# One-hots of queries made by two passes on ScalarE in place of one on VectorE

## The chip, the cores and the metric

The kernel runs on one core of one Trainium2 chip. The metric is the device time of one execution in microseconds (us). Before the change it is 1225.16 us, the median of 14 runs that lie between 1217.1 and 1229.05.

In the profile PE is TensorE (PEld its weight loads), DVE is VectorE, ACT is ScalarE, POOL is GpSimd and SP is SyncE, which issues most of the transfers. Each engine works its own queue of instructions in the order in which the kernel wrote them, and waits on semaphores for data and for free buffers.

## What is computed

One layer of a graph network over 3125 nodes of 128 features and 100000 edges, each of one of 5 types. The edges are sorted by their destination `dst`. For every type r and each of 8 heads:

```
q = x[dst] @ W_Q[r];  k = x[src] @ W_K[r];  v = x[src] @ W_V[r]
logits = (q * k).sum(-1) / 4 + attn_bias[r]            # only edges of type r
attn   = exp(logits - max over the edges of one dst) / (sum over the edges of one dst)
out   += sum over the edges of one dst of attn * v
```

`out` goes through a projection, is added to x and normalised over the features; the result is added to x once more and normalised again.

## The kernel before, in words

**Tables.** In a set-up of about 90 us the kernel makes, per node and type, the keys and values (kv_d) and for the first nodes the queries (q_d, each query as three bf16 parts) in DRAM. It also writes key_d: for every edge its key, 5 times the destination's place in a window plus the type. `row_of` is a column that holds the number of each partition.

**Groups.** The edges are worked in 196 groups of 512 (four tiles of 128 edges). The destinations of a group lie in a window of 25 nodes, so 125 pairs of node and type. A one-hot matrix `hot` of 125 rows by 512 edges says which pair each edge belongs to. A product of `hot` with the window's queries (qw) gives every edge its query (qe); a second product with the window's maxima (mw) gives every edge its maximum. A second one-hot, `at`, with edges along the partitions, sums weighted values over the pairs.

**Steps.** A loop in Python runs over steps k and writes the instructions of all engines in a fixed order; nothing is reordered later. In step k the stages stand for different groups, and the letters v and g name the later and the earlier front of the work:

- SP loads the keys kt (L367, three buffers) and the queries qw (L373) of group k + 3, and mw (L853) for groups whose maxima are due. POOL gathers keys and values of the edges with four indirect transfers a group (L681, into 22 buffers).
- ACT: `by_node` (L949) puts finished sums into place, `carry` copies a window's sums to pt (L930), parts of new queries are cast (L702, L712, L722), `exps` (L876) makes the exponentials, `weights` (L889) and `types` (L753) copy small columns, and `places` makes `at`: four passes of Abs with a bias column (L901) and one Relu over all four tiles (L904).
- PE: `spread_m` (L863) gives the edges their maxima, `sums` (L915, L917 for the carried part from pt, L924) sums, `spread_q` (L746) gives the edges of group k + 1 their queries.
- DVE: `weigh` (L881) weighs values, `less_max` (L872) subtracts the maxima, `norm` (L936 den, L937, L939) divides, `logits` (L759, L760) multiplies queries and keys, and `spot` (L737) makes `hot` of group k + 2 with one comparison of kt against `row_of`. `hot` has 21 buffers, since the same one-hot is used again when the maxima are known, 19 steps later for most groups.

**Blocks.** The maxima are made for blocks of 128 nodes. About every eight steps the logits of a block are complete. POOL loads them by node (ell, L772). ACT turns them to by_head (L787), DVE makes the maxima in three steps (wl at L810, mx at L816, the bf16 parts up to L831). They are stored to m_d (L839) and come back as mw. Once a block also come the projection (L956, L957), the residual and norms on DVE (L974 to L1007), and on ACT the square root (L982), which lies between two loads of ACT's function table.

In the order of a step `spot` stands after `logits`, and `places` after `spot`. The last parts of a step are the parts of queries on DVE (L726, L717), the maxima (with by_head on ACT), the projection and the square root.

Of the kernel before, what the change touches and what calls it, by code (L numbers as in the profile page):

```python
# [11 lines left out]
AF = mybir.ActivationFunctionType  # L12
ALU = mybir.AluOpType
# [33 lines left out]
WR = WN * R  # L47
# [67 lines left out]
def block_of(g, ends=tuple(P * (b + 1) for b in range(NT))):  # L115

    return min(
        b for b, n in enumerate(ends)
        if n >= N or E // N * n - slack(n) >= min(E, (g + 1) * GE)
    )  # L120
# [12 lines left out]
def windowed_path(  # L133
# [4 lines left out]
    nc = tc.nc  # L138
# [90 lines left out]
    def iota(name, pattern, n, base=0, mult=0, dt=F32, pool=const):  # L229
        t = pool.tile([P, n], dt, name=name)  # L230
        nc.gpsimd.iota(
            t, pattern=pattern, base=base, channel_multiplier=mult,
            allow_small_or_imprecise_dtypes=True,
        )
        return t

    node = iota("node", [[P, NT]], NT, mult=1)
    row_of = iota("row_of", [[0, 1]], 1, mult=1)
    row_at = iota("row_at", [[1, P]], P)
    step = iota("step", [[1, P]], P, mult=-1, pool=load)  # L240
    slot = iota("slot", [[1, D]], D)
# [20 lines left out]
    off = load.tile([1, NT], F32, name="off")  # L262
# [89 lines left out]
    live = {}  # L352
# [12 lines left out]
    def fetch_keys(g):  # L365
        kt = ahead.tile([P, T, P], BF16, name="kt")
        nc.sync.dma_start(kt.rearrange("w t p -> w (t p)"), key_d[g].partition_broadcast(P))  # L367
        live["kt", g] = kt

    def fetch_q(g):  # L370
        qw = ahead.tile([P, 3, H], BF16, name="qw")
        f = window(g, first5, SPE)
        nc.sync.dma_start(qw.rearrange("w s h -> w (s h)"), q_d[bass.ds(f, P), :])  # L373
        live["qw", g] = qw
# [303 lines left out]
    def gather(g):  # L678
        kv = kvs_[g % KVB]
        for t in range(T):  # L680
            nc.gpsimd.indirect_dma_start(  # L681
                out=kv[:, t, :], out_offset=None, in_=kv_d[:, :],
                in_offset=bass.IndirectOffsetOnAxis(ap=idx[:, t, g : g + 1], axis=0),
            )


    def fetch_x(name, b):
        n = min(P, N - b * P)
        xb = flow.tile([P, H], F32, name=name, bufs=2 if name == "xq" else 3)
        if n < P:  # L690
            nc.vector.memset(xb, 0.0)
        nc.sync.dma_start(xb[:n], x[b * P : b * P + n, :])
        live[name, b] = xb
# [34 lines left out]
    def store_q(b):  # L728
        live.pop(("xT", b))
        nc.sync.dma_start(  # L730
            q_d[b * P * R : (b + 1) * P * R, :].rearrange("(p r) c -> p (r c)", r=R),
            live.pop(("q3", b)).rearrange("p r s h -> p (r s h)"),
        )

    def spot(g):
        hot = hold.tile([WR, T, P], BF16, name="hot")
        nc.vector.tensor_scalar(hot, live.pop(("kt", g))[:WR], row_of[:WR], None, op0=ALU.is_equal)  # L737
        live["hot", g] = hot

    def spread_q(g):  # L740
# [23 lines left out]
    def store_logits(g):  # L764
        nc.sync.dma_start(
            lg_d[g * GE : (g + 1) * GE, :].rearrange("(p t) c -> p (t c)", t=T),
            live["lg", g].rearrange("p t c -> p (t c)"),
        )
# [81 lines left out]
    def fetch_m(g):  # L850
        mw = late_flow.tile([P, 2, 3, HEADS // 2], BF16, name="mw", bufs=4)
        f = window(g, first5, SPE)
        nc.sync.dma_start(mw.rearrange("w h s k -> w (h s k)"), m_d[bass.ds(f, P), :])  # L853
        live["mw", g] = mw
# [36 lines left out]
    def places(g, on_dve):  # L891

        at = late_flow.tile([P, T, WR], F32, name="at", bufs=3)
        for t in range(T):
            if t < on_dve:
                nc.vector.tensor_scalar(
                    at[:, t, :], row_at[:, :WR], nkey[:, t, g : g + 1], 0.0,
                    op0=ALU.add, op1=ALU.is_equal,
                )
            else:  # L900
                nc.scalar.activation(  # L901
                    at[:, t, :], row_at[:, :WR], AF.Abs, bias=nkey[:, t, g : g + 1], scale=1.0
                )
        nc.scalar.activation(at[:, on_dve:], at[:, on_dve:], AF.Relu, bias=1.0, scale=-1.0)  # L904
        live["at", g] = at
# [21 lines left out]
    def carry(g):  # L927
        if g < NGR - 1:
            pt = late_flow.tile([WR, PW], F32, name="pt")
            nc.scalar.copy(pt, live["pp", g])  # L930
            live["pt", g] = pt
# [15 lines left out]
    def by_node(g):  # L947
        f = window(g, first, ACTE)
        nc.scalar.copy(oT[:, bass.ds(f, WN)], live.pop(("op", g)))  # L949
# [63 lines left out]
    def store_z(b):  # L1013
        n = min(P, N - b * P)
        nc.sync.dma_start(out[b * P : b * P + n, :], live.pop(("z", b))[:n, :])
# [7 lines left out]
    final = step_of[NGR - 1]  # L1023
# [9 lines left out]
    at_k, k = {}, 0  # L1033
    for v in range(NGR):
        k = max(k + 1, ready[block_of(v, MEND)])
        at_k[v] = k
    v_at = {k: v for v, k in at_k.items()}
# [24 lines left out]
    for k in range(-2, root_at[NT] + 2):  # L1062
        v, g = v_at.get(k), group_at.get(k)
        q_step = {k - f: b for b, f in enumerate(q_from) if b >= QB and -2 <= k - f <= 5}

        if k >= 0 and k + 3 in group_at:
            fetch_keys(group_at[k + 3])
            fetch_q(group_at[k + 3])
        if -2 in q_step:
            fetch_x("xq", q_step[-2])  # L1070
        for b in range(NT):
            if done_at[b] - 1 == k:
                fetch_x("xr", b)
            if norm_at[b + 1] + 1 == k:
                store_z(b)
        if 5 in q_step:
            store_q(q_step[5])
        for u in range(NGR):
            if max(at_k[u] - 3, ready[block_of(u, MEND)] - 2) == k:
                fetch_m(u)  # L1080

        while gathered < NGR - 1 and step_of[gathered + 1] <= k + (AHEAD if k < final - 16 else 1):
            gathered += 1
            gather(gathered)
        for b in range(NM):
            if full_step[b] + 1 == k:
                maxima_load(b)

        for b in range(NT):
            if done_at[b] + 1 == k:  # L1090
                residual(b)
        if v_at.get(k - 4) is not None:
            by_node(v_at[k - 4])
        if v_at.get(k - 2) is not None:
            carry(v_at[k - 2])
        if 1 in q_step:
            turned(q_step[1])
        if 3 in q_step or 4 in q_step:
            second_part()
        if 2 in q_step or 3 in q_step:  # L1100
            first_part()

        if v_at.get(k + 1) is not None:
            spread_m(v_at[k + 1], 8 if k + 1 in group_at else 12)
        if v_at.get(k - 1) is not None or v_at.get(k - 3) is not None:
            sums(v_at.get(k - 1), v_at.get(k - 3))
        if k + 1 in group_at:
            spread_q(group_at[k + 1])

        if v is not None:  # L1110
            weigh(v)
        if v_at.get(k + 1) is not None:
            less_max(v_at[k + 1])
            exps(v_at[k + 1])
        if v is not None:
            weights(v)
        if k + 1 in group_at:
            types(group_at[k + 1])
        if v_at.get(k - 2) is not None:
            norm(v_at[k - 2])  # L1120
        if g is not None:
            logits(g)
            store_logits(g)
        if k + 2 in group_at:
            spot(group_at[k + 2])
        if v_at.get(k + 1) is not None:
            places(v_at[k + 1], 2 if k >= final - 1 else 0)
        if 3 in q_step or 4 in q_step:
            third_part()
        if 2 in q_step or 3 in q_step:  # L1130
            remainder()
        for b in range(NM):
            whole = MB[b][2] is None
            last = ready[b] - (3 if whole else 4)
            if last - 2 == k and whole:
                maxima(b, 0, 2)
            if last - 1 == k and whole:
                maxima(b, 2, 4)
            if last == k:
                maxima(b, 4 if whole else 0, R)  # L1140
                store_m(b)
        for b in range(NT):
            if done_at[b] == k:
                project(b)
        for b in range(NT + 1):
            if root_at[b] == k:
                roots(b)
            if norm_at[b] == k:
                norms(b)
        if 0 in q_step:  # L1150
            turn_q(q_step[0])
        if 1 in q_step:
            queries(q_step[1], 0, RH)
        if 2 in q_step:
            queries(q_step[2], RH, R)
# [505 lines left out]
```

## Time and profile before

| | |
|---|---|
| Median of 14 runs | 1225.16 us |
| The profiled execution's own time | 1217.63 us |
| Its span, first to last instruction | 1215.8 us |
| Granted clock of TensorE, mean | 0.804 |
| hot on DVE (L737) | 196, mean 370 ns, 72.4 us busy |
| Abs of places on ACT (L901) | 744, 125 elements each, mean 398 ns |
| Relu of places on ACT (L904), 500 elements | 176, mean 620 ns |
| Gathers on POOL (L681) | 784, mean 950 ns |

A row of a group of instructions gives their number, the time that they kept the engine busy, the mean time of one, and the idle time of the engine just ahead of them with what ended it. A row of a wait gives who waited for whom, the total in us, how many times and the longest. The chain of work that ended last is followed back from the last instruction; its shares say on which engine the time of that one chain was spent, which differs from busy time.

### The profile page before, as it was taken

Reading aid. Unit: us, or ns where it says so; the run is one execution under the profiler, and the core shown is the slowest. Engines: PE = TensorE matmul, PEld = TensorE weight load, DVE = VectorE, ACT = ScalarE, POOL = GpSimd, SP = SyncE. Lnnn points to the kernel's source line nnn. Section 1 sums busy time; section 2 is a strip of 40 time slices with the busy share of each in tenths; the row PEclk is TensorE's granted clock in tenths of the full one; section 3 lists DMA queues with packets and bytes.
Section 4 is the critical chain, followed back from the end, with each engine's and each line's share of the span. In section 5 each row is a group of like instructions: output and inputs, shape, how many; then the busy total and the mean of one; then the engine's idle time right before and its main releaser. Section 6 shows DMA issues by size and latency. Waiting matters only on the chain.

```text
span 1215.8 us, 25674 instructions
## 1 busy us (share of the span) xinstructions
PE 839.6 (69%) x7526; PEld 659.2 (54%) x7526; DVE 931.4 (77%) x2559; ACT 631.1 (52%) x2248; POOL 799.8 (66%) x901
## 2 busy tenths in 40 slices
PE   7984345766667776776678677667767866866794
PEld 3543234655555565565556565546546655655573
DVE  4654377689778878877887897788788788778786
ACT  2560024455664664665565466466556545655453
POOL 1627777777777777776777777777776777667200
PEclk9995558778977888888797878789788778777797
DMA  6887677666766776776676667666666657666300
GB/s 168 323 328 203 165 166 178 180 164 161 193 170 166 179 174 154 171 187 163 161 183 171 154 171 183 162 164 179 171 163 173 180 146 175 174 143 155 73 7 19
DMA packets 180889, 203.63 MB, mean 167 GB/s; under 512 B 83207, under 2 KB 146083, under 8 KB 180620
## 3 DMA queue, kind: packets, MB, share of 16 engines
q0 software_dynamic: 40896, 113.39, 34.1%
q1 hardware_dynamic: 135414, 83.80, 28.4%
q10 hardware_dynamic: 4430, 4.71, 1.6%
q8 instruction: 63, 1.03, 0.3%
q14 instruction: 86, 0.70, 0.2%
HBM read 166.50 MB, written 35.28 MB: 166 GB/s over the span
## 4 chain that ended last, share of the span: by engine, by line
DVE 26%; PE 24%; DMA 17%; ACT 10%; issue 10%; POOL 9%; SPq 3%; ACTq 0%; DVEq 0%; POOLq 0%
POOL kv L681 8%; PE pp L915 8%; DMA mw<-m_d 8%; DMA kv<-kv_d,idx 5%; DVE wl L810 4%; PE pr L395 4%; PE me L863 4%; ACT at L901 4%; DVE prod L759 3%; DVE wv L881 3%; DVE lg L760 3%; DVE mx L816 3%; PE qe L746 2%; DMA qw<-q_d 2%; PE pp L917 2%
## 5 line engine op out<-in xcount | busy, mean ns | idle before, releaser
L681 POOL DMA_INDIRECT kv<-kv_d,idx x784 | 744.9, 950 | 264.3 <-issue 197.3
L915 PE MATMUL pp<-wv,at 128*125 128x136 f32 x1568 | 344.3, 352 | 1.3 <-DVE o L939 1.3
L915 PEld LDWEIGHTS pp<-wv,at 128*125 128x125 f32 x1568 | 258.0, 228 | 60.7 <-issue 58.5
L901 ACT ACTIVATE at<-row_at,nkey 128x125 f32<-128x125 f32 x744 | 237.6, 398 | 0.0
L863 PE MATMUL me<-mw,hot 125*128 125x64 bf16 (+1 forms) x2352 | 124.0, 208 | 152.4 <-DMA mw<-m_d 109.6
L746 PE MATMUL qe<-qw,hot 125*128 125x128 bf16 x2352 | 196.4, 244 | 37.1 <-DVE hot L737 33.4
L876 ACT ACTIVATE me<-me 128x32 f32<-128x32 f32 x196 | 35.7, 182 | 343.9 <-DVE me L872 343.6
L863 PEld LDWEIGHTS <-hot 125*128 125x128 bf16 x2352 | 110.0, 107 | 182.2 <-issue 106.3
L746 PEld LDWEIGHTS <-hot 125*128 125x128 bf16 x2352 | 182.8, 118 | 43.1 <-DVE hot L737 41.1
L759 DVE TENSOR_TENSOR prod<-kv,qe 128x512 f32<-128x512 f32 x196 | 133.0, 679 | 48.8 <-DMA kv<-kv_d,idx 47.0
L760 DVE TENSOR_REDUCE lg<-prod 128x32 f32<-128x512 f32 x196 | 134.4, 686 | 6.8
L881 DVE TENSOR_TENSOR wv<-kv,me 128x512 f32<-128x512 f32 x196 | 132.5, 676 | 3.9 <-PE pp L915 3.9
L917 PE MATMUL pp<-pt,carried 125*5 125x136 f32 x390 | 90.2, 319 | 58.4 <-ACT pt L930 56.5
L904 ACT ACTIVATE at<-at 128x500 f32<-128x500 f32 (+1 forms) x196 | 117.3, 599 | 6.2
L707 PE MATMUL prq<-wq,xTq 128*128 128x384 f32 (+1 forms) x88 | 47.0, 627 | 91.3 <-DVE rem L717 91.3
L872 DVE TENSOR_TENSOR me<-lg,me 128x32 f32<-128x32 f32 x196 | 37.4, 191 | 75.8 <-PE me L863 67.5
L810 DVE TENSOR_TENSOR wl<-by_head,shut 128x1024 f32<-128x1024 f32 (+2 forms) x73 | 76.9, 1053 | 11.0 <-ACT by_head L787 8.5
L816 DVE TENSOR_REDUCE mx<-wl 128x16 f32<-128x1024 f32 (+2 forms) x73 | 76.5, 1048 | 2.5
L924 PEld LDWEIGHTS pp<-rsum,o 125*128 125x128 f32 x392 | 74.5, 232 | 4.1 <-issue 4.0
L737 DVE TENSOR_SCALAR hot<-kt,row_of 125x512 bf16<-125x512 bf16 x196 | 72.4, 370 | 1.5 <-DMA kt<-key_d 1.0
L917 PEld LDWEIGHTS pp<-pt,carried 125*5 125x5 f32 x390 | 18.2, 86 | 97.2 <-ACT pt L930 74.9
L924 PE MATMUL pp<-rsum,o 125*128 125x25 f32 x392 | 67.8, 255 | 3.9 <-DVE o L939 3.9
(184 smaller groups left out, 984.8 us busy)
## 6 DMA issues: line engine op xcount, KB each, us to landing
kt<-key_d SPq DMA_DIRECT2D x196, 128.0 KB
qw<-q_d SPq DMA_DIRECT2D x196, 96.0 KB
kv_d<-kvs SPq DMA_DIRECT2D x24, 640.0 KB
kv<-kv_d,idx POOLq DMA_INDIRECT x784
q_d<-q SPq DMA_DIRECT2D x22, 480.0 KB
lg_d<-lg SPq DMA_DIRECT2D x196, 18.0 KB
mw<-m_d SPq DMA_DIRECT2D x196, 6.0 KB
xr<-in_x SPq DMA_DIRECT2D x24, 64.0 KB
```

Of the source, the lines that this page charges most:

```text
L681: nc.gpsimd.indirect_dma_start(out=kv[:, t, :], out_offset=None, in_=kv_d[:, :], in_offset=bass.IndirectOffsetOnAxis(ap=idx[:, t, g : g + ...
L746: nc.tensor.matmul(qe[:, t, :], hot[:, t, :], qw[:WR, s, :], start=(s == 0), stop=(s == 2))
L759: nc.vector.tensor_tensor(prod, kv[:, :, :H], live.pop(("qe", g)), op=ALU.mult)
L760: nc.vector.tensor_reduce(lg[:, :, :HEADS], prod.rearrange("p t (k d) -> p t k d", d=HD), AX.X, ALU.add)
L810: nc.vector.tensor_tensor(wl, by_head[:, None].to_broadcast([P, n, nh, D]), shut[:, :n, None, :].to_broadcast([P, n, nh, D]), op=ALU.add,)
L863: nc.tensor.matmul(me[:, t], hot[:, t, :], mw[:WR, None, :, s, :].to_broadcast([WR, times, 2, HEADS // 2]), start=(s == 0), stop=(s == 2),)
L881: nc.vector.tensor_tensor(wv[:, :, :H].rearrange("p t (k d) -> p t k d", d=HD), kv[:, :, H:].rearrange("p t (k d) -> p t k d", d=HD), live ...
L901: nc.scalar.activation(at[:, t, :], row_at[:, :WR], AF.Abs, bias=nkey[:, t, g : g + 1], scale=1.0)
L904: nc.scalar.activation(at[:, on_dve:], at[:, on_dve:], AF.Relu, bias=1.0, scale=-1.0)
L915: nc.tensor.matmul(pp, at[:, t, :], wv[:, t, :], start=(t == 0), stop=(t == T - 1))
L917: nc.tensor.matmul(pp[:R], carried[:WR, g, :], live.pop(("pt", g - 1)), start=False, stop=False,)
L924: nc.tensor.matmul(op, live.pop(("o5", done)), rsum[:WR], start=True, stop=True)
```

## The change

`spot` of the first two groups stays as it is, on DVE. From the third group on ACT makes `hot` with two passes. The first overwrites kt with |kt - row|: Abs with the new column `row_neg`, minus the number of the partition, as bias. The second writes Relu(1 - |kt - row|) to `hot`: keys and rows are whole numbers, so that this ramp is 1 at the target and 0 elsewhere. In the order of a step `places` now stands ahead of `spot`, so that on ACT the pair follows the five passes of `places`.

```diff
     row_of = iota("row_of", [[0, 1]], 1, mult=1)
+    row_neg = iota("row_neg", [[0, 1]], 1, mult=-1)
...
     def spot(g):
         hot = hold.tile([WR, T, P], BF16, name="hot")
-        nc.vector.tensor_scalar(hot, live.pop(("kt", g))[:WR], row_of[:WR], None, op0=ALU.is_equal)
+        off = live.pop(("kt", g))[:WR]
+        if g < 2:
+            nc.vector.tensor_scalar(hot, off, row_of[:WR], None, op0=ALU.is_equal)
+        else:
+            nc.scalar.activation(off, off, AF.Abs, bias=row_neg[:WR], scale=1.0)
+            nc.scalar.activation(hot, off, AF.Relu, bias=1.0, scale=-1.0)
         live["hot", g] = hot
...
             store_logits(g)
+        if v_at.get(k + 1) is not None:
+            places(v_at[k + 1], 2 if k >= final - 1 else 0)
         if k + 2 in group_at:
             spot(group_at[k + 2])
-        if v_at.get(k + 1) is not None:
-            places(v_at[k + 1], 2 if k >= final - 1 else 0)
         if 3 in q_step or 4 in q_step:
```

## The prediction

> **What bounds the kernel now.** I read the page first, for shares and the chain; then the waits by size; then one block's instructions in order of time on ACT, DVE and PE.
>
> From the page:
>
> ```profile
> span 1215.8 us, 25674 instructions
> PE 839.6 (69%) x7526; PEld 659.2 (54%) x7526; DVE 931.4 (77%) x2559; ACT 631.1 (52%) x2248; POOL 799.8 (66%) x901
> DVE 26%; PE 24%; DMA 17%; ACT 10%; issue 10%; POOL 9%; SPq 3%; ACTq 0%; DVEq 0%; POOLq 0%
> ```
>
> DVE is the busiest engine, but it carries only 26% of the chain: no engine bounds the kernel alone, the chain goes round all of them. Next, the waits (who waited for whom: us in total, times, longest):
>
> ```profile
> ACT me L876 <- DVE me L872: 343.6, 170, 7.6
> POOL kv L681 <- issue: 197.3, 647, 0.5
> PEld pp L917 <- ACT pt L930: 74.9, 82, 2.3
> DVE prod L759 <- DMA kv<-kv_d,idx: 47.0, 19, 5.5
> DVE den L936 <- ACT pt L930: 14.9, 19, 1.2
> DVE wl L810 <- ACT by_head L787: 8.5, 22, 0.4
> ```
>
> ACT waits 343.6 us for DVE, so on the average it has room. But three rows have somebody waiting for ACT, and two of them come about once a block of nodes (19 and 22 times for 25 blocks). POOL's row says that its gathers run back to back, 0.95 + 0.30 us each: 784 + 25 of them fill 1011 of the 1045 us from 89.1 to 1134.8, which leaves 34 us to be won at most. Now ACT in the block that ends at 648 us (start us, us, instruction, idle time before it):
>
> ```profile
> 612.95 0.18 ACT L876 ACTIVATE me<-me 128x32 f32<-128x32 f32 x1 [1.61 <-DVE me L872]
> ...
> 614.51 0.62 ACT L904 ACTIVATE at<-at 128x500 f32<-128x500 f32 x1
> ...
> 615.86 0.18 ACT L876 ACTIVATE me<-me 128x32 f32<-128x32 f32 x1 [0.27 <-DVE me L872]
> ...
> 618.04 1.28 ACT L982 ACT_TABLE_LOAD   x1
> ...
> 619.60 0.27 ACT L930 COPY pt<-pp 125x136 f32<-125x136 f32 x1
> 619.89 1.28 ACT L876 ACT_TABLE_LOAD   x1
> ...
> 624.43 0.18 ACT L876 ACTIVATE me<-me 128x32 f32<-128x32 f32 x1 [0.83 <-DVE me L872]
> ...
> 625.99 0.62 ACT L904 ACTIVATE at<-at 128x500 f32<-128x500 f32 x1
> 626.52 1.07 ACT L787 COPY by_head<-ell 128x512 f32<-128x512 f32 x1
> ```
>
> and DVE and PE in the same block:
>
> ```profile
> 619.90 0.17 DVE L936 TENSOR_SCALAR den<-pp 125x8 f32<-125x8 f32 x1 [0.77 <-ACT pt L930]
> ...
> 627.62 1.23 DVE L810 TENSOR_TENSOR wl<-by_head,shut 128x1024 f32<-128x1024 f32 x1 [0.44 <-ACT by_head L787]
> ...
> 642.01 0.20 DVE L831 TENSOR_TENSOR m<-mx,m 128x40 bf16<-128x40 f32 x1
> ...
> 648.34 0.80 PE L863 MATMUL me<-mw,hot 125*128 125x64 bf16 x12 [3.31 <-DMA mw<-m_d]
> ```
>
> From 612.95 to 627.6 ACT works almost without a gap: exps and places of four steps, the square root between two table loads, then by_head. DVE waits for its end (0.44), makes the maxima until 642.2, they go out and back as mw, and PE (3.31 idle) starts the next block on them at 648.3. So these four steps of ACT are on the path, once a block.
>
> **The change, part by part.** *Removed:* 194 of 196 one-hots on DVE. One takes 0.34 us and delays what follows by 0.26 (next start less its own, 632.65 to 632.91). Between 627.6 and 642.0 there are two on the path: -0.52 us a block. In the four steps before, DVE waits for ACT anyway, and in the two after, PE waits for mw: nothing.
>
> *Added:* a pair of passes on ACT a step. The second, Relu of 512 elements, is priced by the places' Relu of 500: 0.620, so 0.63. The first has a bias column; the nearest row is the count's Sign (250 elements, bias column, 0.506), and the places' 250 and 500 rows (0.412, 0.620) give 0.83 ns an element, so 0.506 + 262 x 0.00083 = 0.72. Between a pass and the one that reads it lie 0.03 us (L901's end to L904), and an unrelated successor starts 0.09 before the end (625.99 + 0.53). A pair delays ACT by 0.72 + 0.03 + 0.54 = 1.29 us. Bounds: 1.06 (two at L904's pitch, 0.53) and 1.40 (0.72 twice less overlap); I take 1.29, nearest to both kinds of pass.
>
> The Trainium skill (ScalarE: Activation LUTs, Rules for kernel authors) sends relu-like work to VectorE and calls DVE "up to about 3× faster in bf16". By that ratio alone a pass would be an estimated 3 x 0.34 = 1.03 us, a pair 2.06, and the block sum below 6.6 instead of 3.5 us. I go by the rows, which put one pass at about twice DVE's one-hot.
>
> *On the path, block 605 to 648:* delay after the first step 1.29; the idle 0.27 at 615.86 takes some back, 1.02; after the second step 2.31. That goes through the table load and square root into pt at 619.60, and DVE, which waits there already, waits 2.31 more. After the third step 3.60. At 624.43 the idle 0.83 goes: DVE's own part comes 2.31 - 0.26 later and is still ahead of ACT; 2.77. After the fourth step 4.06, which by_head and then DVE's wl take in full. Less 0.52: **+3.5 us in this block**. Called a sum: 4 x 1.29 - 1.10 - 0.52. The same sum on the rows of the blocks whose by_head ends at 456.7, 584.9, 843.4 and 1017.9 gives 3.3, 2.4, 3.3 and 1.6; the mean of the five is 2.8. In the other four steps the waits of L876 for DVE (2.80, 2.86, 2.15, 2.72) hide the pair, as long as they stay over 1.29.
>
> Seventeen blocks (by_head from 413.6 to 1099.2) have this form: 17 x 2.8 = 48. Five before have POOL still behind: DVE waits there for kv (9.8 and 2.4 us in the first two) and covers the delay; in the other three I count 2 each, 6. The last block's wl doesn't wait for by_head. Sum: **+54 us**.
>
> *The rest, together:* The constant's iota on POOL (another of that shape took 0.12) lies in the set-up, before the gathers at 89 us. The move of spot behind places changes ACT's order alone: on DVE's queue places has work only from the step where no spot is left. The new waits on ACT are those that spot had on DVE, with by_node, pt and exps of the next step queued behind: for kt, loaded a step and more ahead (DVE waited for it once, 1.0 us), and for hot's buffer. No DMA is issued by spot. It frees kt for SP's load three groups on, and SP has two steps for that. The buffer of hot is that of 21 groups before, whose last readers on PE ended at least 6.2 us before the places of that step. PE's wait for hot can't be longer than the one for pt, which ACT now makes just after the pair and PE needs ahead of it. The first 15 steps have no places: ACT idles and POOL sets the pace, so nothing. The last 20 have no spots.
>
> Own time of the profiled run: 1217.6 (span 1215.8 and 1.8 around it), so 1272; it is one of the lowest of 14 and the median is 7.5 above it: **1225 + 54 = 1279 us**.
>
> **Rivals.** (a) *Faster: DVE's relief counts and ACT has room.* For it: 77% against 52% busy, and 343.6 us of ACT waiting for DVE. The Trainium skill (Perfetto Trace Analysis, Identifying the Most-Contended Engine) says to optimise the engine of highest occupancy first; by that all 194 x 0.344 would count, an estimated -67 us. The gathers leave only 34. If the pairs are hidden, the three one-hots on the chain of a block go (those at 614.78, 632.65, 638.31: 0.26 each), 0.78 x 22 = 17: 1208 us. It decides if a pair is under (1.10 + 0.52) / 4 = 0.4 us; against it, one bf16 cast of 384 elements takes 0.51 on ACT. (b) *Slower, less:* the pair is at its lower bound, and PE, less pressed, gets a clock over the present 0.80, which shortens its pieces of the chain (some 9 us a block) by 5%: 17 x (2.8 - 0.8 - 0.45) + 6 = 32, some 1240 to 1257. (c) *Slower, more:* pairs of the later steps come out too, because pt late holds PE (82 waits already) and that holds qe and DVE. One more pair a block is 17 x 1.29 = 22: 1301; all four would be 88: 1367. Against it: those idle times of 2 to 3 us. (d) *The change doesn't do what it says:* the two functions could need table loads of their own; the places use both 940 times between exps without one, so I leave it at nothing.
>
> **How the numbers follow.** Main case 0.70, with its own range 1260 to 1300 (pair 1.06 to 1.40, and 1.6 to 3.5 us a block); (b) 0.08; (c) 0.13, mostly under 1325; (a) 0.07; no change 0.02. The range 1243 to 1318 holds the main case, most of (b) and two thirds of (c). Within 0.3%, about what a measurement of this kernel tells from no change, only a chance meeting of (a) and (b) would fall.
>
> **What would show it.** Right: two ACT rows in place of L737, near 0.72 and 0.63 us, 194 each; DVE's wait at wl for by_head up from 0.4 to about 4 us a time, and at den for pt from 0.8 to about 3; the gap from one by_head to the next up from some 43 us to 46; POOL idle for freed buffers. DVE's busy time falls by 67 us and ACT's rises by some 250, to about 70%. Wrong: wl's wait under 1 us, or a pair well under 1 us (then a or b); L876 no longer waiting in the later steps (then c).

## The result, and the profile after

| | before | after |
|---|---|---|
| Median of the runs | 1224.43 us (47 runs, 1216.51 to 1232.24) | 1271.55 us (10 runs, 1268.05 to 1274.84) |
| Ratio, 95% interval | | 1.0389 [1.0367, 1.0411] |
| Profiled execution, own time | 1217.63 us | 1279.67 us |
| Its span | 1215.8 us | 1277.9 us |

The kernel became 47 us slower. The two profiled executions lie 62 us apart: that of before is one of the fastest of its kernel, that of after lies above all ten runs. For that reason the differences that are read from the two traces add up to 62 us and not to the 47 of the medians. Line numbers of the loop are 1 to 6 higher after the change.

The page after:

```profile
span 1277.9 us, 26125 instructions
PE 882.9 (69%) x7526; PEld 697.1 (55%) x7526; DVE 881.1 (69%) x2365; ACT 862.8 (68%) x2636; POOL 799.6 (63%) x902
DVE 20%; PE 19%; DMA 19%; ACT 18%; POOL 11%; issue 10%; SPq 2%; ACTq 0%; DVEq 0%; POOLq 0%
L742 ACT ACTIVATE kt<-kt,row_neg 125x512 bf16<-125x512 bf16 x194 | 137.2, 707 | 21.8 <-DMA kt<-key_d 19.8
L743 ACT ACTIVATE hot<-kt 125x512 bf16<-125x512 bf16 x194 | 122.1, 630 | 6.1
```

DVE is 50 us less busy and ACT 232 us more; the four engines' shares are now nearly alike, none is over 70%, and the kernel is slower. ACT's share of the chain went from 10% to 18%. The waits after (who waited for whom: us in total, times, longest):

```profile
ACT me L882 <- DVE me L878: 256.5, 130, 7.0
POOL kv L682 <- issue: 199.9, 654, 0.6
PEld pp L923 <- ACT pt L936: 170.1, 102, 3.3
DVE den L942 <- ACT pt L936: 82.6, 61, 2.5
POOL kv L682 <- DVE den L942: 56.3, 42, 3.9
DVE prod L765 <- DMA kv<-kv_d,idx: 49.9, 20, 5.3
DVE wl L816 <- ACT by_head L793: 38.8, 22, 3.0
ACT kt L742 <- DMA kt<-key_d: 19.8, 9, 4.0
```

The three rows in which somebody waits for ACT grew from 74.9 to 170.1, from 14.9 to 82.6 and from 8.5 to 38.8 us. DVE alone waits 98 us more for ACT, and POOL now waits 56 us at den, which is DVE's place in its queue when it is late in freeing gather buffers (10.5 us before). The last row is new: ACT waits nine times for the keys, each time ahead of 166 us, when the gathers hold DVE up too.

Now ACT in the block whose by_head ends at 658.9 us (start us, us, instruction, idle time before it):

```profile
640.49 0.18 ACT L882 ACTIVATE me<-me 128x32 f32<-128x32 f32 x1 [1.60 <-DVE me L878]
...
642.05 0.62 ACT L910 ACTIVATE at<-at 128x500 f32<-128x500 f32 x1
642.58 0.71 ACT L742 ACTIVATE kt<-kt,row_neg 125x512 bf16<-125x512 bf16 x1
643.31 0.63 ACT L743 ACTIVATE hot<-kt 125x512 bf16<-125x512 bf16 x1
...
644.27 0.20 ACT L882 ACTIVATE me<-me 128x32 f32<-128x32 f32 x1
...
647.75 1.28 ACT L988 ACT_TABLE_LOAD   x1
...
649.60 1.28 ACT L882 ACT_TABLE_LOAD   x1
...
654.47 0.20 ACT L882 ACTIVATE me<-me 128x32 f32<-128x32 f32 x1
...
656.57 0.70 ACT L742 ACTIVATE kt<-kt,row_neg 125x512 bf16<-125x512 bf16 x1
657.31 0.63 ACT L743 ACTIVATE hot<-kt 125x512 bf16<-125x512 bf16 x1
657.84 1.06 ACT L793 COPY by_head<-ell 128x512 f32<-128x512 f32 x1
```

and DVE in the same block:

```profile
644.41 0.17 DVE L942 TENSOR_SCALAR den<-pp 125x8 f32<-125x8 f32 x1 [1.31 <-ACT pt L936]
...
649.61 0.17 DVE L942 TENSOR_SCALAR den<-pp 125x8 f32<-125x8 f32 x1 [2.41 <-ACT pt L936]
...
654.62 0.17 DVE L942 TENSOR_SCALAR den<-pp 125x8 f32<-125x8 f32 x1 [0.77 <-ACT pt L936]
...
658.94 1.23 DVE L816 TENSOR_TENSOR wl<-by_head,shut 128x1024 f32<-128x1024 f32 x1 [1.70 <-ACT by_head L793]
...
672.63 0.20 DVE L837 TENSOR_TENSOR m<-mx,m 128x40 bf16<-128x40 f32 x1
```

The idle times at 615.86 and 624.43 (0.27 and 0.83) are gone: their counterparts, the exps at 644.27 and 654.47, start with no wait. From the first exps to the end of by_head the stretch takes 658.90 - 640.49 = 18.41 us, before 627.59 - 612.95 = 14.64: 3.77 longer. DVE waits four times in it, 6.19 us together, before twice, 1.21. From by_head's end to the end of the maxima it is 672.83 - 658.90 = 13.93, before 14.62: 0.69 shorter; the two one-hots that DVE no longer makes there are 0.52 of it.

Over many blocks, on the first and the last by_head of sixteen blocks before and after:

```profile
367.66 1.07 ACT L787 COPY by_head<-ell 128x512 f32<-128x512 f32 x1
...
1059.88 1.06 ACT L787 COPY by_head<-ell 128x512 f32<-128x512 f32 x1
```

```profile
381.20 1.06 ACT L793 COPY by_head<-ell 128x512 f32<-128x512 f32 x1
...
1116.29 1.07 ACT L793 COPY by_head<-ell 128x512 f32<-128x512 f32 x1
```

A block takes (1059.88 - 367.66) / 16 = 43.26 us before and (1116.29 - 381.20) / 16 = 45.94 after: +2.68. Of the 62 us between the two traces these sixteen blocks hold 42.9; the five blocks ahead of them 12.7, what lies ahead of the first by_head 0.8, and what comes after the last of the sixteen 5.6.

Where in a block? The steps are numbered back from `ready`, the step at which a block's maxima are due. The table is worked out from the DVE rows of less_max (its start to that of the next) in both traces, as the mean of those sixteen blocks. (Its rows begin and end half a block later than the sixteen intervals above, so that their sums differ a little from 43.26 and 45.94.)

| step | -8 | -7 | -6 | -5 | -4 | -3 | -2 | -1 | sum |
|---|---|---|---|---|---|---|---|---|---|
| before, us | 3.19 | 3.41 | 5.41 | 6.39 | 5.69 | 6.31 | 6.57 | 6.19 | 43.15 |
| after, us | 2.95 | 3.87 | 6.68 | 8.22 | 5.44 | 6.13 | 6.48 | 6.22 | 45.99 |

Three steps got longer, by 0.46, 1.27 and 1.83 us. They are those that lie between ACT's exps of ready - 8 and by_head, which ACT makes at the end of ready - 5. The two steps behind by_head got shorter, by 0.25 and 0.18, and the step -8 by 0.24: about one of DVE's one-hots each.

### The profile page after: what moved, and what is told of

It reads as the page before. It is cut to its first block, busy times and chain, and to the rows that moved or that the text cites. A ratio compares the mean times of both kernels' runs of the same rounds, so it can differ in the third digit from the quotient of the medians.

```text
span 1277.9 us, 26125 instructions
## 1 busy us (share of the span) xinstructions
PE 882.9 (69%) x7526; PEld 697.1 (55%) x7526; DVE 881.1 (69%) x2365; ACT 862.8 (68%) x2636; POOL 799.6 (63%) x902
## 4 chain that ended last, share of the span: by engine, by line
DVE 20%; PE 19%; DMA 19%; ACT 18%; POOL 11%; issue 10%; SPq 2%; ACTq 0%; DVEq 0%; POOLq 0%
POOL kv L682 11%; DMA kv<-kv_d,idx 9%; PE pp L921 6%; DMA mw<-m_d 6%; ACT at L907 5%; PE pr L396 3%; DVE wl L816 3%; ACT at L910 3%; DVE prod L765 3%; ACT kt L742 3%; PE me L869 3%; DVE lg L766 2%; DVE wv L887 2%; DVE mx L822 2%; PE qe L752 2%
## 5 line engine op out<-in xcount | busy, mean ns | idle before, releaser
L921 PE MATMUL pp<-wv,at 128*125 128x136 f32 x1568 | 361.9, 365 | 0.0
L921 PEld LDWEIGHTS pp<-wv,at 128*125 128x125 f32 x1568 | 272.6, 240 | 63.3 <-issue 62.5
L752 PE MATMUL qe<-qw,hot 125*128 125x128 bf16 x2352 | 209.3, 253 | 40.0 <-DVE prod L765 31.0
L752 PEld LDWEIGHTS <-hot 125*128 125x128 bf16 x2352 | 196.3, 124 | 44.9 <-issue 28.4
L869 PE MATMUL me<-mw,hot 125*128 125x64 bf16 (+1 forms) x2352 | 130.3, 214 | 123.7 <-DMA mw<-m_d 88.2
L869 PEld LDWEIGHTS <-hot 125*128 125x128 bf16 x2352 | 117.7, 111 | 152.7 <-issue 108.0
L923 PE MATMUL pp<-pt,carried 125*5 125x136 f32 x390 | 94.4, 332 | 147.6 <-ACT pt L936 146.9
L765 DVE TENSOR_TENSOR prod<-kv,qe 128x512 f32<-128x512 f32 x196 | 133.0, 678 | 51.6 <-DMA kv<-kv_d,idx 49.9
L742 ACT ACTIVATE kt<-kt,row_neg 125x512 bf16<-125x512 bf16 x194 | 137.2, 707 | 21.8 <-DMA kt<-key_d 19.8
L743 ACT ACTIVATE hot<-kt 125x512 bf16<-125x512 bf16 x194 | 122.1, 630 | 6.1
L923 PEld LDWEIGHTS pp<-pt,carried 125*5 125x5 f32 x390 | 18.2, 86 | 188.9 <-ACT pt L936 170.1
L816 DVE TENSOR_TENSOR wl<-by_head,shut 128x1024 f32<-128x1024 f32 (+2 forms) x73 | 76.9, 1053 | 41.3 <-ACT by_head L793 38.8
L942 DVE TENSOR_SCALAR den<-pp 125x8 f32<-125x8 f32 x196 | 31.6, 161 | 82.9 <-ACT pt L936 82.6
L930 PEld LDWEIGHTS pp<-rsum,o 125*128 125x128 f32 x392 | 79.8, 247 | 4.2 <-issue 4.1
```

Source lines behind the costliest of these rows:

```text
L742: nc.scalar.activation(off, off, AF.Abs, bias=row_neg[:WR], scale=1.0)
L743: nc.scalar.activation(hot, off, AF.Relu, bias=1.0, scale=-1.0)
L752: nc.tensor.matmul(qe[:, t, :], hot[:, t, :], qw[:WR, s, :], start=(s == 0), stop=(s == 2))
L765: nc.vector.tensor_tensor(prod, kv[:, :, :H], live.pop(("qe", g)), op=ALU.mult)
L816: nc.vector.tensor_tensor(wl, by_head[:, None].to_broadcast([P, n, nh, D]), shut[:, :n, None, :].to_broadcast([P, n, nh, D]), op=ALU.add,)
L869: nc.tensor.matmul(me[:, t], hot[:, t, :], mw[:WR, None, :, s, :].to_broadcast([WR, times, 2, HEADS // 2]), start=(s == 0), stop=(s == 2),)
```

## The experiments

**The theories.** Theory 1 is the prediction's: the pair costs only in the four steps from ready - 8 to ready - 5, where ACT is on the path, and in the others it hides in ACT's wait for DVE. Theory 2: it costs by its load, wherever it stands, for instance because pt comes late to PE in every step.

**1. Pairs in the last four steps only.**

```diff
+    early = {r - i for r in ready for i in range(5, 9)}
...
-        if g < 2:
+        if on_dve:
             nc.vector.tensor_scalar(hot, off, row_of[:WR], None, op0=ALU.is_equal)
...
-            spot(group_at[k + 2])
+            spot(group_at[k + 2], k < 0 or k < ready[0] or k in early)
```

> The pair runs on ACT only in the last four steps of each block (ready - 4 to ready - 1); in the other four, and in the first 16 steps, DVE makes the one-hot as before. Theory 1 (the pair costs only where ACT is on the path, from the exps eight steps ahead of ready to by_head, and there in full): no cost is left, and DVE keeps the 0.52 us a block that it saves between by_head and the maxima, 17 x 0.52 = 9 us: 1225 - 9 = 1216 us, 1212 to 1222; DVE's wait at wl for by_head stays near 0.4 us a time. Theory 2 (ACT's added load costs alike in any step, for instance by pt coming late to PE): half of the measured 47 us, about 1248 us.

Measured: 1214.25 us against 1225.52 of the kernel before on the same chip, ratio 0.9931 [0.9899, 0.9963]: faster than before by 11 us, with 88 pairs on ACT.

```profile
DVE den L942 <- ACT pt L936: 20.5, 21, 1.2
DVE wl L816 <- ACT by_head L793: 9.6, 21, 1.2
```

DVE's two waits for ACT stay near those of before (14.9 and 8.5 us). In the steps -4 and -3 the block got shorter by 0.29 and 0.25 us, in the steps -8 to -5 its sum is 0.1 longer than before. Theory 2 wanted 1248.

**2. Pairs in the first four steps only.** The same, with `k < 0 or k not in early` for the choice of DVE.

> The reverse: the pair runs on ACT only in the four steps from ready - 8 to ready - 5 and in the first steps; DVE makes the one-hot in ready - 4 to ready - 1. Theory 1: the whole cost stays and DVE's saving of some 9 us goes, 1272 + 9 = 1281 us, 1272 to 1288: slower than the changed kernel, though it has half of its pairs. Theory 2: about 1248 us.

Measured: 1278.47 us, ratio 1.0468 [1.0418, 1.0518]. It is slower than the changed kernel, with 94 of its 194 pairs.

```profile
DVE den L942 <- ACT pt L936: 84.6, 60, 2.5
DVE wl L816 <- ACT by_head L793: 36.2, 23, 3.1
```

The two waits are close to those of the changed kernel (82.6 and 38.8). So the whole loss comes from the pairs in these steps, and by the medians the others had been giving some of it back. In the trace that shows in the steps -4 and -3 alone (5.66 and 6.32 us, 5.44 and 6.13 with the change); the block as a whole takes 46.03 us, against 45.94. Theory 2, which wanted 1248 both times, falls. The one-hots of the first steps outside the four are on DVE here, unlike in the description above: 12 of the 194 pairs stand on ACT in neither experiment.

**3. The pair after carry.** All pairs stay on ACT, in the same steps, at another place of ACT's order.

```diff
         if v_at.get(k - 2) is not None:
             carry(v_at[k - 2])
+        if k + 2 in group_at:
+            spot(group_at[k + 2])
...
         if v_at.get(k + 1) is not None:
             places(v_at[k + 1], 2 if k >= final - 1 else 0)
-        if k + 2 in group_at:
-            spot(group_at[k + 2])
```

> All pairs on ACT as in the changed kernel, but the pair of a step stands behind carry and ahead of exps, where it stood behind places; one-hots are made for the same group in the same step. Theory 1: the first pair of the stretch now falls into ACT's wait for DVE, so three in place of four lie on the path, 1.29 us a block less: 1272 - 17 x 1.29 = 1250 us, 1242 to 1260, and DVE's waits at den for pt get shorter (82.6 us in all with the change). Theory 2 (load): no change, about 1272 us. A third: the exps get late by the pair in every step, and the kernel is slower than 1272 us.

Measured: 1248.5 us, ratio 1.0198 [1.0151, 1.0246]: half of the loss is gone by place alone.

```profile
DVE den L942 <- ACT pt L936: 41.5, 42, 2.4
DVE wl L816 <- ACT by_head L793: 38.1, 23, 3.1
```

DVE's wait for pt is half of the changed kernel's, that for by_head is the same. The block's mean in its trace is 44.76 us, 1.18 less than with the change, where 1.29 was expected. ACT's idle time ahead of the exps of ready - 8 fell from 1.65 to 0.33 us, which is the first pair gone into it. This order also puts pt ahead of the pair in each step, and it makes ACT wait more for the keys (76.1 us in 44 times); in the block of that trace whose by_head starts at 640.15 the wait, 1.41 us, lies in the step -1, ahead of exps that wait for DVE after it all the same.

**4. The stretch itself shortened.** If ACT's stretch sets the block, then taking something else out of it must help, with and without the pairs. The square root with its two table loads, and the norms that DVE makes on it, go four steps later.

```diff
-    root_at = {b: d + 2 for b, d in done_at.items()}
+    root_at = {b: d + (6 if d + 6 < final - 1 else 2) for b, d in done_at.items()}
```

On the kernel before:

> The kernel before, with the square root and the norms of a block four steps later (root at done + 6 in place of done + 2), so that the two table loads of 1.28 us and the root leave ACT's stretch ahead of by_head, and DVE's norms leave it too. No one-hot moves. Theory 1 (ACT's stretch sets the block): by_head comes about 2.3 us a block earlier, 17 x 2.3 = 39 us, of which POOL's gathers allow some 34: about 1195 us, 1185 to 1208, and DVE's wait at wl goes. Theory 2 (the stretch is not what counts): 1225 us.

Measured: 1209.71 us against 1227.19 on the same chip, ratio 0.9859 [0.9831, 0.9888]: 17 us faster where 30 were expected. What the root and its loads give, and what DVE's norms give, was not told apart.

On the changed kernel:

> The changed kernel with the same later root. Theory 1: with 2.86 us less in the stretch the four pairs come out at some +0.9 us a block against the kernel before in place of +2.8: about 1240 us, 1230 to 1250. Theory 2 (the pairs cost by load, not by place): 1272 us as with the change.

Measured: 1231.93 us, ratio to the kernel before 1.0035 [1.0005, 1.0066]. The pairs cost 47 us with the root in the stretch and 22 (1231.93 - 1209.71) with the root out of it. The number of pairs is the same in both. The time lies in theory 1's range. But theory 1 had put the two kernels with the later root at 1195 and 1240, 45 us apart, and they are 22 apart, since the one without pairs had gained less than expected. In its trace ACT stands idle for 1.66 and 1.77 us ahead of the exps of the steps -6 and -5; with the pairs that is 0.01 and 0.56. So the pairs take up idle time that the later root had opened.

With the pairs of experiment 1:

> The pair on ACT only in the last four steps of a block, and the later root. Theory 1: the gain of the first is left only as far as POOL's gathers leave room: between 1185 and 1200 us, and not slower than the later root alone. Theory 2: the pairs now share their steps with the root and its two table loads, so that a second stretch forms on ACT, and the kernel is slower than with the later root alone, by 1 us a block or more (over 1215 us).

Measured: 1204.38 us, ratio 0.9822 [0.9793, 0.9850]. It is the fastest kernel on the chips used so far, 1.8% ahead of the kernel before. It is 5 us ahead of the later root alone, and just over the upper end of what was expected (1200).

**5. What limited the later root?** Theory 1 had wl's wait go, and 2.3 us a block with it. The block in that trace got shorter by 0.44 (43.26 to 42.83), and wl waits still. That trace explains little of the gain: it lies only 4 us below that of before, where the medians lie 17 apart. With the later root on the kernel before:

```profile
DVE me L872 <- PE me L863: 82.6, 57, 3.8
DVE wl L810 <- ACT by_head L787: 6.1, 17, 0.5
DVE den L936 <- ACT pt L930: 2.7, 5, 1.2
```

The wait for pt went as it should (14.9 to 2.7 us). The wait of less_max for PE came instead: 67.5 us in 35 times before, 82.6 in 57 now. By steps it is 1.06 and 1.28 us in the steps -6 and -5, where it was 0.37 and 0.10, and PE waits there for mw; in the step -1 it fell from 2.64 to 1.14. The step -6 got 0.98 shorter, the step -7 0.68 longer, from 3.41 to 4.09. Two theories were to be told apart by fetching mw a step earlier:

```diff
-            if max(at_k[u] - 3, ready[block_of(u, MEND)] - 2) == k:
+            if max(at_k[u] - 4, ready[block_of(u, MEND)] - 2) == k:
                 fetch_m(u)
```

> The kernel before with the later root, and mw fetched four steps ahead of its use in place of three (never ahead of ready - 2). The later root alone gave 17 us of the 30 expected; in its trace DVE's less_max waits for PE's me 1.06 and 1.28 us a block in the steps ready - 6 and ready - 5, where it waited 0.37 and 0.10 before, and PE waits there for mw. Theory G (the gain was given back to mw, which now comes late in the quick steps): up to 17 x 1.9 = 32 us more, as far as POOL's gathers allow (89 + 1011 + 81 after the last + 2 = 1183 us): 1186 to 1202 us. Theory F (POOL's gathers are the bound with the later root already): no change, 1210 us.

> The pair on ACT in the last four steps of a block only, the later root, and mw fetched a step earlier. Theory G: 1204 less up to 20 us, 1184 to 1197 us. Theory F: 1204 us.

A third kernel with the earlier mw had by_head's copy in a function of its own, `heads`, ahead of places:

```diff
+        for b in range(NM):
+            if ready[b] - (5 if MB[b][2] is None else 4) == k:
+                heads(b)
         if v_at.get(k + 1) is not None:
             places(v_at[k + 1], 2 if k >= final - 1 else 0)
```

> As the run before this one, and by_head's copy stands ahead of places on ACT instead of behind it, so that DVE's wl no longer waits for it (0.44 us a block before). If ACT's place in the order still counts, 17 x 0.4 = 7 us less than that run; if POOL's gathers or PE bound it by then, the same time within 3 us.

Measured: 1587.0, 1612.86 and 1616.99 us, against 1619.13 us of the kernel before on that chip (ratios 0.9775 [0.9728, 0.9822], 0.9962 [0.9929, 0.9996], 0.9981 [0.9947, 1.0016]). On this chip the kernel before itself was a third slower than on those of the runs so far. In the trace of the first of the three:

```profile
PEld L863 <- issue: 246.7, 184, 6.2
POOL kv L681 <- DVE den L936: 232.4, 53, 9.3
DVE me L872 <- remote: 209.5, 28, 15.3
```

PE stands still inside its products for no reason that the profile shows (the first row was 106.3 us before), and DVE waits up to 15 us for something that the profile doesn't name. Three more runs on other chips:

> The later root with mw fetched a step earlier, on another chip: on the last one the kernel before itself took 1619 us, its DMAs and waits being much longer, so that its runs can't be set beside the others. Theory G (gain of the later root given back to late mw): ratio to the kernel before 0.97 to 0.98, 1190 to 1202 us, and DVE's less_max waits in ready - 6 and ready - 5 fall from 1.06 and 1.28 us to under 0.5 each. Theory F (POOL's gathers bound it): 0.986 as with the later root alone.

> The same with the pair on ACT in the last four steps of a block. Theory G: 0.965 to 0.978, 1184 to 1198 us, where the same without the earlier mw gave 0.982. Theory F: 0.982.

> The pair on ACT in the last four steps of a block, the later root, and mw a step earlier, once more in the hope of a chip on which the kernel before takes its 1225 us. Without the earlier mw it was 1204 us, 0.982. Theory G (late mw takes back part of the gain): 0.965 to 0.978, 1184 to 1198 us, and DVE's less_max waits in the steps ready - 6 and ready - 5 fall from 0.72 and 1.38 us to under 0.5 each. Theory F (POOL's gathers, or another path, bound it): 0.982 and the time that is saved in those waits comes back elsewhere.

Measured: 1625.56 and 1630.85 us against 1650.1 (0.9882 [0.9831, 0.9932] and 0.9816 [0.9761, 0.9871]), then 1617.78 against 1615.42 (1.0017 [0.9980, 1.0053]). On these chips too the kernel before was a third slower. The same kernel gave 0.996, 0.982 and 1.002 there, and the later root without the earlier mw was not run on such a chip. So these six runs tell nothing of the two theories: why the later root gave 17 us in place of 30 stays open. That mw comes late in the shortened steps is seen in the trace and not shown to be the cause.

## Why the prediction was right, and where it was off

**The sum.** Predicted 1279 us with the range 1243 to 1318; measured 1271.55. Against the runs shown with the prediction the sum was +54 us, measured +47. The block, the term that carries it, was +2.8 us predicted and +2.68 in the traces, at the place that was named: experiments 1 and 2 show that the pairs of the first four steps make the whole loss.

**The pair.** 0.72 + 0.63 us and 1.29 us of delay predicted; the rows have 0.707 and 0.630, and from the first pass at 656.57 to by_head at 657.84 it is 1.27. The ratio of a pass to DVE's 0.344 us is 2.1 and 1.8: the rule's "up to about 3×" (the Trainium skill, ScalarE: Activation LUTs, Rules for kernel authors) holds as a bound, and the estimate by it, 6.6 us a block, would have been more than twice the measured.

**The stretch.** For one block 4.06 us predicted, 3.77 measured; both idle times were used up as predicted.

**DVE's waits.** The total was right and its division wrong. The prediction had wl's wait at about 4 us a time; it is 38.8 / 22 = 1.8. It had DVE wait 2.31 more at the den after the root, and then counted the delay in full once more at wl, as if DVE were on time there. But what DVE waits at den it doesn't wait again at wl, and it is held at den three times a block (1.31, 2.41 and 0.77; the prediction named one, at about 3). 6.19 - 1.21 = 4.98 us more waiting, less the four one-hots that DVE no longer makes there (in the rows of before they delay what follows by 0.26, 0.46, 0.25 and 0.26, together 1.23), gives 3.75; by_head comes 3.77 later.

**DVE's saving.** Predicted 0.52 us a block between by_head and the maxima; 0.69 in the block shown. The busy time of DVE was to fall by 67 us and fell by 50: the step at fault is 194 x 0.344, which counts each one-hot in full though it overlaps its neighbours; 50 / 194 is 0.26 us, what one delays its successor by in the prediction's own row. By ACT's busy time some 250 were predicted, 232 measured, 1.19 us a pair, for the same overlap.

**The early blocks.** Predicted nothing for the first two, which the wait for kv was to cover, and 2 each for the other three, 6 us; the traces give 2.8 for the two and 9.9 for the three, 2.5 a block as in the later ones. DVE's wait for kv went on (47.0 us before, 49.9 after), but 37 and 44 us of it lie ahead of the second by_head. The cover was taken to reach further than it does. And 5.6 us come out after the last of the sixteen blocks, where the prediction had counted one more block of 2.8. These two terms explain why the traces lie further apart than the sum. The medians lie less far apart than either; how their 47 us divide over the terms was not measured, and that the sum came within 7 us of them is in part luck. For the keys the prediction counted no wait; there are the 19.8 us above, all in the first 166 us, ahead of all but the first by_head.

**The later steps.** The idle time ahead of the exps, which was to hide the pair, went from 2.79, 2.94, 2.32 and 2.88 us (mean of the steps -4 to -1) to 2.83, 1.42, 1.83 and 2.45. The pair of each step eats into the idle time of the next and leaves some in all four, and experiment 1 shows that pairs there cost nothing.

**Rivals.** (a) A pair takes 1.27 us, far over the 0.4 below which (a) was to hold. But its idea is right for half of the steps: experiment 1 is the faster kernel that it described. The rule that it leaned on, to optimise the engine of highest occupancy first (the Trainium skill, Perfetto Trace Analysis, Identifying the Most-Contended Engine), is not borne out by itself here: DVE's occupancy went from 77% to 69% and the time rose 3.9%. (b) gave PE a higher clock; it was lower (see below). In its sum four pairs at the lower bound are 4 x (1.29 - 1.06) = 0.92 us less, not 0.8, which is 2 us in all. (c) is out by experiments 1 and 2. (d) is out: the trace of after has the same table loads as that of before, 21 at the square root and 20 at the exps.

## What to carry to other kernels

An engine's busy share says little of what a move onto it costs: ACT, 52% busy and waiting 344 us for DVE, had one stretch of four steps a block with almost no idle time, and all of the loss came from the pairs in it. Look for such a stretch by following who waits for the engine, not for whom it waits: two rows of 15 and 8 us, about once a block each, named it. The same work in the other four steps was a gain, and something else taken out of the stretch (two table loads and a root on ACT, norms on DVE) was worth more than the one-hots.

## What was not expected of the hardware

The granted clock of TensorE was lower with the change, 0.763 to 0.782 in its runs against 0.78 to 0.80 in those of the kernel before, though PE did the same products over a longer time; the products L915 took 365 ns on the mean after and 352 before. It is not what made the kernels slow: the profiled run of experiment 2 was granted 0.804, as that of before, and took 1273.93 us against 1217.63. Whether the lower clock has a share in the changed kernel's 47 us is open.

On some chips the kernel before took 1615 to 1650 us instead of 1225. In the trace of the first kernel with the earlier mw the single instructions of DVE, ACT and POOL take the same time as on the other chips (a gather's issue 948 ns, prod 677, the Relu of places 599 in both), while the products L915 take 372 ns; the clock is granted at 0.69 to 0.72 in the runs of the kernel before, and the time goes into waits that the profile puts down to "issue" or "remote". Its DMA packets take no longer, unlike what the expectation of the next run of the same kernel, on another chip, says of it: those of the two main queues fill 47.4% of 1588.2 us, 753 us, and before 62.5% of 1215.8, 760. What differs on those chips is open.
